# A gated attention and expert block: later groups measured before the token loop, the second norm scaled on ACT one step later

## The chip, the cores and the metric

The kernel runs on one core of a Trainium2 chip. The metric is the device time of one execution in microseconds, as the median of several runs. Engines are named as in the profile: PE multiplies matrices, DVE works on vectors, ACT applies functions, POOL (GpSimd) does small vector work and issues indirect transfers, and SP issues the plain ones.

## The reference, cut to what matters

Two residual blocks over 2048 tokens of width 256. The first is attention with 16 heads over a sliding window, whose keys and values come from a context; the second is a mixture of eight experts of which each token takes two. Each starts with a norm over the width, and each is gated by the tanh of one number:

```python
def _layernorm(x, axis=-1, eps=1e-05):
    m = jnp.mean(x, axis=axis, keepdims=True)
    v = jnp.var(x, axis=axis, keepdims=True)
    return (x - m) / jnp.sqrt(v + eps)

x = x + jnp.tanh(g_xattn[0]) * _L0_xattn_ref(_layernorm(x), ctx_1024, ctx_1024, wq, bq, wk, bk, wv, bv, wo, bo)
x = x + jnp.tanh(g_ffn[0]) * _L0_ffn_ref(_layernorm(x), ln_gamma, ln_beta, Wr, W12, W3)

# in _L0_ffn_ref, which norms its input once more:
xn = (xf - mu) / jnp.sqrt(var + 1e-05) * ln_gamma + ln_beta
logits = jnp.clip(xn @ Wr.T, -CLAMP, CLAMP)
probs = softmax(logits); top_p, top_i = jax.lax.top_k(probs, 2)
# each expert has a buffer of 640 slots; a token takes the next free one of each of its two experts
buf = jnp.zeros((E, cap, D)).at[e_s, pos].set(xn[t_s], mode='drop')
gu = einsum('ecd,efd->ecf', buf, W12); h = silu(gu[..., :D_FF]) * gu[..., D_FF:]
y = einsum('ecf,edf->ecd', h, W3)        # then weighted and added to the token's row
```

## The kernel before, in words

**Tiles and groups.** The tokens are cut into 16 tiles of 128 (`NB`), four tiles to a group (`NG` = 4 groups). One pass of the loop over `t` (L958) is called a step. It does the attention of tile t in three layers at once: it finishes tile t, whose scores were made one step earlier; it makes the scores of tile t + 1 and their exponents; and it takes tiles t - 1 and t - 2 through the output projection, the second norm and the router.

**A step, in the order written.** `summed(t, 1)` adds up the second half of the exponents (DVE, `sm`, L541). `divided(t - 1)` (L602 to L612) spreads the inverted sums over the heads on PE, copies them on ACT (`rb`) and multiplies on DVE (`oT`). `inverted(t)` (L543) takes the reciprocal on DVE (`rd`) and splits it on POOL into three parts of bf16 by four small operations (`rp`, L549 to L552). `scores(t + 1)` and `largest` follow (PE `ps`, DVE `mx`, L522), then `turned(t, 0)`: eight transposes on PE and two copies on ACT (`prT`, L563). Then, for t >= 2, `facing(t - 2)` transposes the normed tile (PE, `pxt`, L673) and `facing_read` copies it (ACT, `x2T`, L680). `attended(t - 1)` is the output projection (PE, L618). `attended_read(t - 1)` adds it to `x` on DVE (L631), takes mean and variance (L635, L637), and prepares the norm's factor: `ve` on DVE (L639), `rs`, its power of -1/2, on POOL (L643). After `turned(t, 1)` comes a unit of projection work for later tiles (`units(t)`, L730: keys, queries, values or turned rows, in one or two parts), the router's matmuls `routed(t - 2)` (L685) and `by_head(t)` (L575), which turns `rp` on PE; `by_head_read` copies it on DVE (`rdT`). `weighted(t)` (`po`, L591) is the product with the values.

**The second norm.** Near the end of step t, `scaled(t - 1)` subtracts the mean and multiplies by `rs` on DVE (`h2`, L650), then multiplies by gamma and adds beta on POOL (L659, L660). The last of these is returned as `normed`.

**The first norm of later groups.** Step t, for t = 1 to 8, measures one tile of group g + 2 (`measured`, L331: DVE bn_stats, bn_aggr, ve, and the power on POOL), and at its end scales it (`normed_x`, L345, `xn`) and adds the projection's bias to `x` (`biased`, L359, POOL).

**The router's sends.** When the slots of some tiles are known (`chosen`, `ranked`, `placed`, for tiles 0 to 2, 3 to 6, 7 to 10, 11 to 13 and 14, 15), each tile has two indirect transfers to make (`send`, L862, on POOL), 32 in all. `pace(normed, n)` (L949) issues up to n of them, queued behind `normed`. Three groups of tiles are sent within the loop; the rest follow it. The first expert's rows are fetched early by SP (L1027), after the sends that are out by step 12, and turned by the units `faced` (L700) in step 14.

**What sets the order.** The loop stands in `tc.manual_schedule(engines={PE, ACT, DVE})`: these three engines run their instructions as written. POOL and SP are ordered by a planner when the kernel is built; a send may not go ahead of its `normed`. PSUM banks for passing results come from one pool of three, taken in turn (`bank`, L90): a bank is reused as soon as the third one after it is asked for, and the taker waits until it was read.

**After the loop** (L1121 on), the last two tiles go through the same stations while PE starts on the first expert with the rows already fetched. The experts' part (from L1187) is not touched.

Of the kernel before, what the change touches and what calls it, by code (L numbers as in the profile page):

```python
# [20 lines left out]
P = 128  # L21
D = 256
DC = D // P
NB = 16
# [12 lines left out]
CAP = 640  # L37
# [18 lines left out]
def flamingo_block(  # L56
# [264 lines left out]
    with tc.tile_pool(name="grp", bufs=2) as grp, tc.tile_pool(  # L321
# [305 lines left out]
        def attended_read(t, pp):  # L627
            g, b = divmod(t, GB)
            x1 = xs[g][:, b, :]

            nc.vector.scalar_tensor_tensor(x1, pp, tgx[:, 0:1], x1, ALU.mult, ALU.add)  # L631


            st = small.tile([P, 6], F32, tag="st1", name=f"st1_{t}")
            nc.vector.bn_stats(st, x1)  # L635
            mv = small.tile([P, 2], F32, tag="mv1", name=f"mv1_{t}")
            nc.vector.bn_aggr(mv, st)  # L637
            ve = small.tile([P, 1], F32, tag="ve1", name=f"ve1_{t}")
            nc.vector.tensor_scalar(  # L639
                ve, mv[:, 1:2], 1.0 + LN_EPS, LN_EPS * LN_EPS, ALU.mult, ALU.add  # L640
            )
            rs = small.tile([P, 1], F32, tag="rs1", name=f"rs1_{t}")
            nc.gpsimd.tensor_tensor(rs, ve, minus_half[:, 0:1], ALU.pow)  # L643
            return mv, rs

        def scaled(t, mv, rs):
            g, b = divmod(t, GB)
            x1 = xs[g][:, b, :]
            h2 = wk.tile([P, D], F32, tag="h2", name=f"h2_{t}")
            nc.vector.tensor_scalar(  # L650
                h2, x1, mv[:, 0:1], rs[:, 0:1], ALU.subtract, ALU.mult
            )
            if b == 0:
                xn2s[g] = nrm.tile([P, GB, ROW], F32, tag="xn2", name=f"xn2_{g}")
                nc.gpsimd.tensor_copy(
                    xn2s[g][:, :, ROW - 1], tok_f[:, g * GB : (g + 1) * GB]
                )
            xn2 = xn2s[g]
            nc.gpsimd.tensor_tensor(h2, h2, ga_sb, ALU.mult)  # L659
            normed = nc.gpsimd.tensor_tensor(xn2[:, b, 0:D], h2, be_sb, ALU.add).ins  # L660
# [62 lines left out]
        def done(unit):  # L723
            parts, evict = unit
            for part in parts:
                part()
            return evict


        def units(t):  # L730
            g, b = divmod(t, GB)
            if t < GB:
                return [
                    lambda: unit_q(1, 0),
                    lambda: unit_q(1, 1),
                    lambda: unit_v(1, (0, 1)),
                    lambda: unit_k(2, 0),
                ][t : t + 1]
            if NB - 5 <= t < NB - 2:
                return [lambda: unit_v(g + (b + 1) // GB, ((t + 1) % GB,))]  # L740
            if t == NB - 2:
                return [lambda: faced((0, 1)), lambda: faced((2,))]
            if t == NB - 1:
                return [lambda: unit_v(g, (b,)), unit_none]
            return [
                [lambda: unit_k(g + 1, 1)],
                [lambda: unit_t(g + 1), lambda: unit_q(g + 1, 0)],
                [lambda: unit_v(g, (2, 3)), lambda: unit_q(g + 1, 1)],
                [lambda: unit_k(g + 2, 0), lambda: unit_v(g + 1, (0, 1))],
            ][b]  # L750
# [150 lines left out]
        with tc.manual_schedule(engines={PE, ACT, DVE}):  # L901
# [31 lines left out]
            nc.scalar.activation(tgx, gx_sb, AF.Tanh)  # L933
            for oc in range(DC):
                done(unit_q(0, oc))()
            sc = scores(0)
            for q in range(2):
                largest(0, q, sc)
# [19 lines left out]
            for t in range(NB):  # L958
# [4 lines left out]
                if t == 0:  # L963
                    prTs = turned(t, 0, sc)
                    parts, evict = unit_t(1)
                    parts[0]()
                    scn = scores(t + 1)
                    parts[1]()
                    evict()
                    summed(t, 1, sc)  # L970
                    rd = inverted(t, sc)
                    for q in range(2):
                        largest(t + 1, q, scn)
                else:
                    summed(t, 1, sc)
                    oT = divided(t - 1, *pend)
                    rd = inverted(t, sc)
                    if nxt:
                        scn = scores(t + 1)
                        for q in range(2):  # L980
                            largest(t + 1, q, scn)
                    prTs = turned(t, 0, sc)
                if t >= 1:
                    if t >= 2:
                        x2T = facing_read(t - 2, facing(t - 2))
                    norm = attended_read(t - 1, attended(t - 1, oT))
                if routing is not None:
                    place = placed(*ranked(*routing))
# [3 lines left out]
                ahead = t >= 1 and t - 1 < GB * (NG - 2)  # L992
                if ahead:
                    g, b = divmod(t - 1, GB)
                    mv_rs = measured(g + 2, [b])
                prTs += turned(t, 1, sc)
                parts, evict = work[0]()
                if len(work) > 1:
                    for part in parts:
# [8 lines left out]
                if t >= 2:  # L1008
                    routed_read(t - 2, pl)
                rdT = by_head_read(t, prd)  # L1010
                po = weighted(t, prTs, rdT)
                pend = po, rdT
                if t == 13:
                    next(choice)
                if routing is not None:
# [1 line left out]
                        pass  # L1017
                    waiting += of_tiles(*routing[0:2])
                    routing = None
                if t >= 1:  # L1020
                    normed = scaled(t - 1, *norm)

                    pace(normed, 3 if t < 11 else 4 if t < 13 else 2)
                if t == KNOWN:
                    assert not waiting
                    after_sent(
                        nc.sync.dma_start(  # L1027
                            rows_a,
                            slot_d[FIRST * CAP : FIRST * CAP + AS, :].rearrange(
                                "(s p) r -> p s r", p=P  # L1030
                            ),
                        ).ins
                    )
                if nxt:
                    exponents(t + 1, 0, H // 4 if t >= 1 else 0, H // 2, scn)
                    summed(t + 1, 0, scn)
                if ahead:
                    normed_x(g + 2, [b], *mv_rs)
                    biased(g + 2, [b])
                if t == KNOWN:  # L1040

# [615 lines left out]
```

## Time and profile before

| what | value |
|---|---|
| median of 3 runs | 509.55 us (509.44 to 509.55) |
| the profiled execution's own time | 510.99 us |
| its span, from first to last instruction | 509.3 us |
| busy PE / DVE / ACT / POOL | 479.6 / 300.3 / 226.4 / 173.0 us |
| the token loop, steps 1 to 15 | 33.1 to 182.4 us of the span |
| one step | 8.7 to 12.1 us |

Times in a profile are microseconds from the span's start. A line such as L643 is a line of the kernel's source. In a window's row, the first figure is its length; then come the busy time and number of instructions of PE, of PE's weight loads, of DVE, ACT and POOL, then the clock granted to PE (1.00 is full), the share of the DMA engines and their GB/s. In the timeline, brackets hold how long the engine had been idle and what released it.

### The profile page before, as it was taken

What the parts mean: (1) busy time and instruction counts of PE and PEld (TensorE: products, weight loads), DVE (VectorE), ACT (ScalarE), POOL (GpSimd) and SP (SyncE); (2) the same over time, 40 slices, a digit from 0 to 9 for tenths busy, and PEclk for the clock granted to TensorE, in tenths of its full rate; (3) what the DMA queues carried; (4) which work ended last, traced back from release to release, by engine and by line L of the source; (5) the groups of instructions that cost most, each with busy time, mean ns of one, the idle gap of its engine ahead of it and who ended that gap; (6) DMA issues with size and microseconds to landing.
All of it is one profiled execution on the core that took longest, in us unless ns stands there. A gap on an engine that the chain in (4) does not pass through costs nothing.

```text
span 509.3 us, 8874 instructions
## 1 busy us (share of the span) xinstructions
PE 479.6 (94%) x3095; PEld 364.9 (72%) x3095; DVE 300.3 (59%) x748; ACT 226.4 (44%) x650; POOL 173.0 (34%) x255
## 2 busy tenths in 40 slices
PE   9989999999988799999999999999999999999992
PEld 4556666667666566788887897987768776877682
DVE  6679997898779757125646373662663366235410
ACT  3689887688786633121221351422440344124300
POOL 6145434284265457302232322233110311034112
PEclk9999999999999999999999999999999999999998
DMA  8999610020022036401839472844700521024301
GB/s 254 328 278 390 235 43 1 2 82 27 1 86 77 18 102 229 160 2 25 308 64 305 116 232 37 267 91 82 266 10 5 130 51 12 4 35 108 132 14 41
DMA packets 38412, 59.21 MB, mean 116 GB/s; under 512 B 3616, under 2 KB 33824, under 8 KB 36192
## 3 DMA queue, kind: packets, MB, share of 16 engines
q1 hardware_dynamic: 30704, 47.71, 27.8%
q0 software_dynamic: 7056, 10.24, 10.6%
q8 instruction: 44, 0.72, 0.6%
q14 instruction: 64, 0.52, 0.4%
q10 hardware_dynamic: 544, 0.00, 0.1%
HBM read 39.40 MB, written 19.34 MB: 115 GB/s over the span
## 4 chain that ended last, share of the span: by engine, by line
PE 66%; DVE 12%; issue 7%; ACT 5%; DMA 5%; POOL 2%; SPq 0%; POOLq 0%; DVEq 0%; ACTq 0%
PE py L1399 16%; PE pg L1343 9%; PE pu L1343 7%; PE pu L1257 4%; PE pg L1257 4%; ACT pr L533 4%; DMA acc_d<-ysb,tok 4%; DVE sm L541 3%; PE pp L561 3%; DVE mx L522 3%; PE bank L1343 3%; PE pk L376 2%; PE pv L451 2%; PE ps L510 2%; PE pg L1090 2%
## 5 line engine op out<-in xcount | busy, mean ns | idle before, releaser
L1425 POOL DMA_INDIRECT acc_d<-ysb,tok x35 | 57.2, 1634 | 186.7 <-DMA acc_d<-ysb,tok 68.2
L1399 PE MATMUL py<-w,hT 128*128 128x256 f32 x432 | 97.1, 379 | 0.0
L1399 PEld LDWEIGHTS py<-w,hT 128*128 128x128 f32 x432 | 80.8, 190 | 11.3 <-DVE hT L1354 0.5
L533 ACT ACTIVATE pr<-ps,mx 128x128 f32<-128x128 f32 x256 | 69.9, 417 | 7.9 <-DVE mx L522 7.8
L1343 PE MATMUL pg<-bufT,w 128*128 128x320 f32 (+1 forms) x160 | 50.6, 398 | 0.2
L563 ACT COPY prT<-pp 128x512 f32<-128x512 f32 x64 | 35.0, 602 | 20.3 <-PE pp L561 20.1
L541 DVE TENSOR_REDUCE sm<-pr 128x8 f32<-128x1024 f32 x32 | 38.8, 1214 | 6.7 <-ACT pr L533 6.5
L1413 DVE TENSOR_SCALAR ysb<-py,rows 128x256 f32<-128x256 f32 x20 | 9.7, 484 | 55.0 <-PE py L1399 45.0
L1236 ACT COPY bufT<-bank 128x256 f32<-128x256 f32 (+1 forms) x42 | 11.4, 347 | 61.5 <-PE bank L1231 54.2
L522 DVE TENSOR_REDUCE mx<-ps 128x8 f32<-128x1024 f32 x32 | 36.7, 1188 | 3.4 <-PE ps L510 3.3
L561 PE MATMUL pp<-ident,pr 128*128 128x128 f32 x256 | 35.6, 282 | 0.3 <-DVE x_all L631 0.3
L1343 PEld LDWEIGHTS pg<-bufT,w 128*128 128x128 f32 x160 | 28.0, 189 | 10.7 <-ACT vp L1377 2.3
L561 PEld LDWEIGHTS pp<-ident,pr 128*128 128x128 f32 x256 | 29.5, 145 | 7.2 <-issue 4.8
L864 POOL DMA_INDIRECT slot_d<-xn,slot x32 | 31.7, 990 | 8.8 <-issue 7.0
L1374 ACT ACTIVATE vp<-pu 128x320 f32<-128x320 f32 (+1 forms) x40 | 15.8, 395 | 29.2 <-PE pu L1343 15.3
L1269 ACT ACTIVATE vp<-pg 128x256 f32<-128x256 f32 x24 | 9.2, 384 | 36.2 <-PE pg L1257 32.7
L1363 ACT COPY pg<-pg 128x320 f32<-128x320 f32 (+1 forms) x20 | 7.3, 367 | 33.6 <-PE pg L1343 29.0
L618 PE MATMUL pp<-wo_sb,oT 128*128 128x256 f32 x64 | 17.9, 403 | 4.3 <-DVE oT L612 2.9
L451 PE MATMUL pv<-wv_sb,ctx 128*128 128x256 f32 x64 | 17.8, 407 | 1.8 <-DVE x_all L631 1.4
L643 POOL TENSOR_TENSOR rs<-ve,minus_half 128x1 f32<-128x1 f32 x16 | 8.9, 558 | 27.9 <-DVE ve L639 26.3
L510 PE MATMUL ps<-keo,qT 32*128 32x256 f32 x256 | 18.4, 401 | 0.0
L591 PE MATMUL po<-prT,vp 128*32 128x128 f32 x512 | 17.4, 276 | 0.0
(227 smaller groups left out, 953.8 us busy)
## 6 DMA issues: line engine op xcount, KB each, us to landing
w<-in_w12T_dram SPq DMA_DIRECT2D x16, 1024.0 KB, 9.5
w<-in_w3T_dram SPq DMA_DIRECT2D x8, 1024.0 KB, 12.5
slot_d<-zrow SPq DMA_DIRECT2D x1, 5300.0 KB, 26.2
rows<-slot_d SPq DMA_DIRECT2D x7, 662.5 KB, 5.6
x_all<-in_x_dram SPq DMA_DIRECT2D x4, 512.0 KB, 6.5
acc_d<-x_all SPq DMA_DIRECT2D x4, 512.0 KB, 3.2
out_dram<-acc_d SPq DMA_DIRECT2D x4, 512.0 KB, 5.7
ctx<-in_ctxT_dram SPq DMA_DIRECT2D x3, 512.0 KB, 5.9
```

What stands on the lines that cost most here:

```text
L451: nc.tensor.matmul(pv[:, i, :], lhsT=cg[:, c, bs[i] * P : (bs[i] + 1) * P], rhs=wv_sb[:, c, :], start=(c == 0), stop=(c == DC - 1),)
L510: nc.tensor.matmul(pss[s // 2][:, s % 2, 2 * oc : 2 * oc + 2, :], lhsT=qT[rows, oc, b * P : (b + 1) * P], rhs=keo[rows, oc, b, :, :], star ...
L522: nc.vector.tensor_reduce(mx, sc[0][q], AX.X, ALU.max, negate=True)
L533: nc.scalar.activation(prs[q][:, i, j, :], pss[q][:, i, j, :], AF.Exp, bias=mxs[q][:, i, j : j + 1],)
L541: nc.vector.tensor_reduce(sc[3][:, q, :, :], sc[2][q], AX.X, ALU.add)
L561: nc.tensor.transpose(ppt[:, j, :], sc[2][q][:, i, j, :], ident)
L563: nc.scalar.copy(prT, ppt)
L864: d = nc.gpsimd.indirect_dma_start(out=slot_d, out_offset=bass.IndirectOffsetOnAxis(ap=slot[:, k, t : t + 1], axis=0), in_=xn2s[g][:, b, : ...
L1257: nc.tensor.matmul(ps, lhsT=w12[:, c, f0 : f0 + P], rhs=(buf[:, c, :, 0 : n // 2] if len(buf.shape) == 4 else buf[:, c, lo - off : hi - off]),
L1343: nc.tensor.matmul(to, lhsT=lhs[:, i * P : (i + 1) * P], rhs=rhs[:, 0:n], start=start, stop=True, skip_group_check=not start,)
L1399: mm = nc.tensor.matmul(py, lhsT=h, rhs=w3[:, f, :], start=(f == 0), stop=(f == FC - 1),)
L1425: nc.gpsimd.indirect_dma_start(out=acc_d, out_offset=bass.IndirectOffsetOnAxis(ap=tok[:, s : s + 1], axis=0), in_=ysb[:, s, :], in_offset= ...
```

## The change

The second norm's `ve` moves from DVE to POOL, which also computes a `shift` of minus mean times `rs`; `h2` becomes one activation on ACT with that shift and scale. `scaled` moves from the end of step t (for tile t - 1) to the beginning of step t + 1, with the sends that are queued behind it, and `facing` of that tile to a place behind the second `turned`. Groups 2 and 3 are measured whole, one ahead of the loop and one in step 0. Around these the number of sends per step, the fetch of the first expert's rows (from step 12 to step 13), the unit `faced((2,))` (from step 14 to step 15) and the order after the loop are fitted.

```diff
             ve = small.tile([P, 1], F32, tag="ve1", name=f"ve1_{t}")
-            nc.vector.tensor_scalar(
+            nc.gpsimd.tensor_scalar(
                 ve, mv[:, 1:2], 1.0 + LN_EPS, LN_EPS * LN_EPS, ALU.mult, ALU.add
             )
             rs = small.tile([P, 1], F32, tag="rs1", name=f"rs1_{t}")
             nc.gpsimd.tensor_tensor(rs, ve, minus_half[:, 0:1], ALU.pow)
-            return mv, rs
-
-        def scaled(t, mv, rs):
+            shift = small.tile([P, 1], F32, tag="shift", name=f"shift_{t}")
+            nc.gpsimd.tensor_scalar(shift, mv[:, 0:1], rs[:, 0:1], -1.0, ALU.mult, ALU.mult)
+            return shift, rs
+
+        def scaled(t, shift, rs):
...
-            nc.vector.tensor_scalar(
-                h2, x1, mv[:, 0:1], rs[:, 0:1], ALU.subtract, ALU.mult
-            )
+            nc.scalar.activation(h2, x1, AF.Identity, bias=shift[:, 0:1], scale=rs[:, 0:1])
...
             if t == NB - 2:
-                return [lambda: faced((0, 1)), lambda: faced((2,))]
+                return [lambda: faced((0, 1))]
             if t == NB - 1:
-                return [lambda: unit_v(g, (b,)), unit_none]
+                return [lambda: unit_v(g, (b,)), lambda: faced((2,))]
...
                 done(unit_q(0, oc))()
+            of_groups = {2: measured(2, every)}
             sc = scores(0)
...
                     summed(t, 1, sc)
                     oT = divided(t - 1, *pend)
+                    if t >= 2:
+                        normed = scaled(t - 2, *norm)
+
+                        pace(normed, 4 if KNOWN <= t < NB - 1 else 3)
+                    if t == KNOWN + 1:
+                        assert not waiting
+                        after_sent(
+                            nc.sync.dma_start(
+                                rows_a,
...
                     rd = inverted(t, sc)
...
                 if t >= 1:
-                    if t >= 2:
-                        x2T = facing_read(t - 2, facing(t - 2))
                     norm = attended_read(t - 1, attended(t - 1, oT))
...
-                    mv_rs = measured(g + 2, [b])
                 prTs += turned(t, 1, sc)
+                if t >= 2:
+                    x2T = facing_read(t - 2, facing(t - 2))
                 parts, evict = work[0]()
...
                 rdT = by_head_read(t, prd)
+                if t == 0:
+                    of_groups[3] = measured(3, every)
                 po = weighted(t, prTs, rdT)
...
-                if t >= 1:
-                    normed = scaled(t - 1, *norm)
-
-                    pace(normed, 3 if t < 11 else 4 if t < 13 else 2)
-                if t == KNOWN:
-                    assert not waiting
-                    after_sent(
...
                 if ahead:
-                    normed_x(g + 2, [b], *mv_rs)
+                    normed_x(g + 2, [b], *(m[:, b : b + 1] for m in of_groups[g + 2]))
                     biased(g + 2, [b])
...
             oT = divided(t, *pend)
-            x2T = facing_read(t - 1, facing(t - 1))
+            normed = scaled(t - 1, *norm)
+            pace(normed, 3)
             c = chosen(t - 4, 3)
             next(c)
             gate_or_up(0, 0)
             next(c)
             norm = attended_read(t, attended(t, oT))
+            x2T = facing_read(t - 1, facing(t - 1))
             silu(0)
```

More of the change, by code (lines that the diff above doesn't have):

```diff
@@ L976, in flamingo_block @@
                     oT = divided(t - 1, *pend)
+                    if t >= 2:
[6 more added lines that the diff above has]
+                                rows_a,
+                                slot_d[FIRST * CAP : FIRST * CAP + AS, :].rearrange(
+                                    "(s p) r -> p s r", p=P
+                                ),
+                            ).ins
+                        )
                     rd = inverted(t, sc)
@@ L1019, in flamingo_block @@
                     routing = None
-                if t >= 1:
-                    normed = scaled(t - 1, *norm)
-                    pace(normed, 3 if t < 11 else 4 if t < 13 else 2)
-                if t == KNOWN:
-                    assert not waiting
-                    after_sent(
[L1027 to L1033, printed above, removed]
                 if nxt:
```

## The prediction

> **What bounds the kernel now.** I read the page first (busy shares), then cut the token-tile loop into its sixteen steps and asked for the busy time of each, then followed the chain of waits through them, then read single steps in the timeline. A step t begins here where `divided(t - 1)` issues its matmuls (L602).
>
> ```profile
> PE 479.6 (94%) x3095; PEld 364.9 (72%) x3095; DVE 300.3 (59%) x748; ACT 226.4 (44%) x650; POOL 173.0 (34%) x255
> ```
>
> Over the whole span PE looks like the only bound, but the change touches only the first 190 us. There the steps differ. The windows below are steps 3, 6, 10, 12 and 15 (length, then busy time and instructions of PE, weight loads, DVE, ACT, POOL, then the granted clock):
>
> ```profile
> 51.05:59.70 8.65, 8.63 (x98) 5.82 (x98) 8.20 (x18) 7.28 (x25) 4.29 (x10) 1.00 0.95 339
> 79.31:90.84 11.53, 10.63 (x106) 7.31 (x106) 9.52 (x26) 8.12 (x27) 4.19 (x10) 1.00 0.01 2
> 122.44:133.16 10.72, 10.67 (x107) 7.32 (x106) 8.08 (x21) 8.04 (x27) 2.86 (x7) 1.00 0.00 0
> 142.48:152.60 10.12, 8.43 (x100) 6.07 (x99) 8.03 (x16) 7.88 (x27) 7.70 (x14) 1.00 0.32 108
> 172.79:182.44 9.65, 7.69 (x66) 6.31 (x66) 5.28 (x14) 5.34 (x17) 5.13 (x10) 0.82 0.08 28
> ```
>
> Steps 6 and 10 carry the same matmuls (their `units` are both V and Q). Step 10 is 10.72 us and all PE; step 6 is 11.53. The 0.8 us between them is DVE, as the chain in step 6 shows (start, time, what):
>
> ```profile
> 81.13 1.13 DVE sm L541
> 82.26 0.33 DVE oT L612
> 82.75 2.20 DVE mx L522 x2
> 84.95 0.40 DVE x_all L631
> 85.40 2.01 PE pv L451 x8
> ```
>
> So steps 1 to 3, 10 and the start of 11 are PE's; 4 to 8 and 13, 14 are lengthened by DVE. Step 12 is neither. In its timeline (start, duration, engine; in brackets the wait before) POOL issues four sends, and only then the casts of the inverted row sums (`rp`), though `rd` was there at 145.55; PE's turn of `rp` (L575) waits 1.33 us:
>
> ```profile
> 143.69 0.73 POOL L660 TENSOR_TENSOR xn<-h,be_sb 128x256 f32<-128x256 f32 x1
> 144.59 1.06 POOL L864 DMA_INDIRECT slot_d<-xn,slot  x1 [0.16 <-issue]
> 145.31 0.24 DVE L545 RECIPROCAL rd<-sm 128x16 f32<-128x16 f32 x1
> ...
> 148.49 0.96 POOL L864 DMA_INDIRECT slot_d<-xn,slot  x1 [0.30 <-issue]
> 149.45 0.21 POOL L549 CAST rp<-rd 128x16 bf16<-128x16 f32 x1
> 150.30 0.22 POOL L552 TENSOR_TENSOR rp<-rest,rp 128x16 bf16<-128x16 f32 x1
> 150.57 0.24 PE L575 MATMUL small<-ident_b,rp 128*48 128x128 bf16 x1 [1.33 <-POOL rp L552]
> ```
>
> **The change, part by part.**
>
> *Measuring groups 2 and 3 at once.* Removed from each of steps 1 to 8: on DVE bn_stats 0.41, bn_aggr 0.18, ve 0.15 (means of L337, L338, L340), 0.74 us; on POOL one pow of 0.56 to 0.73. Added twice: four pairs and one ve; for group 1 that took 12.83 to 15.25, 2.42 us, and its pow 1.01 on POOL. The first copy stands on DVE after group 1's scaling (ends 17.8) and before `mx` of tile 0, which starts at 21.07 after 3.30 us of idling: it ends at 20.2 if x's third load is there. That load is issued at 11.04 and these loads land 5.5 to 7.7 us later, so by 18.7; then 21.1 at worst: nothing. Without that idle time it would cost 2.4. The second copy stands behind tile 0's `rdT` (31.37), where DVE idles 1.06 and then 0.85 us: 2.42 - 1.91 = 0.5 us late for oT and mx of step 1, on the path: +0.5.
>
> *ve to POOL, shift added, h2 to ACT.* DVE loses 0.15 + 0.40 us a step, about 0.55. POOL gains two operations on 128x1; no such row exists. Between its 128x4 copy (0.19) and the 128x1 pow (0.56) I take 0.2 each, as the 128x16 casts cost. They are wanted only a step later: nothing on the path, up to 0.5 us a step more if POOL is full. h2 on ACT has no row either (a scale and a bias per partition from SBUF): the 128x256 copy L680 takes 0.40, the 512 wide one with bias L433 0.78; I take 0.40. It stands behind `rb`, where ACT then waits for PE's transposes anyway (L563 waits 20.1 us over 20 places; step 6: rb ends 80.56, the copy starts 81.91). Nothing; without that cover 14 x 0.4 = 5.6 us.
>
> *What DVE's relief is worth.* 1.3 us a step in 1 to 8, 0.55 later, but only until PE binds. By twins: step 4 to step 3, 0.3; step 6 to step 10, 0.8; step 5 to its twin step 9 (10.14), which itself still waits for DVE, 0.5 to 0.9, say 0.8; step 7 has no twin, 0.4; steps 11 and 14, 0.4 and 0.5. Sum -3.2. There is a rule to weigh: the Trainium skill (SBUF — State Buffer, "SBUF: two separate sides") says that DVE and GpSimd take a shared port pair exclusively for a whole instruction, where DVE runs a two-port mode or reads two SBUF operands. The row: `xn` L350 takes 0.40, but 0.71 while POOL adds beside it (59.40, 68.38). By the row each such meeting costs 0.3 us, and moving POOL's two 0.73 us operations from `xn`'s side to `sm` (1.20 to 1.22 in all 32) and PSUM reads spares perhaps 8 x 0.3 of DVE, 2.4 us; taken literally the lock could hold DVE for the whole 0.73. Neither changes my sum: steps 1 to 8 are then PE's.
>
> *The turn (facing) later in the step.* The same two transposes and one copy. attended comes 0.22 us sooner, facing now needs the bank that attended leaves (DVE's L631), as the unit did before. Where the unit is half a V (steps 11 to 13), its 0.4 us hardly cover x2T's copy: +0.3 us, hidden behind the next point. Zero to +1 in all; I take 0. `faced((2,))` goes from step 14 to 15, PE 0.44 us each way; the wait of 1.05 us for its bank (L673 for L711) may go: 0 to -1.
>
> *The sends move with h2.* Here I expect the loss. Sends are queued behind the norm's last add. Before, this add ran at the end of a step, so three sends were over soon in the next (step 8: 107.4, casts done 6.23 us into the step, PE's need at 7.17). PE, ACT and DVE keep their written order; POOL is ordered by a planner, but in every step of this trace where sends and casts meet, POOL kept the written order, and the new code writes scaled and sends ahead of `inverted`. From a step's beginning: rb ends at 1.2 to 2.5; h2 +0.4; the multiply +0.07; the add 0.81 later; from the add's start to the first cast 4.52 us with three sends (111.84 to 116.36), 5.76 with four (143.69 to 149.45); the casts 1.07. With the old rb ends (2.02, 2.19, 1.36, 1.95, 2.49) `rp` is ready at 8.9, 9.1 (steps 8, 9: three), 9.5, 10.1 (12, 13: four) and 9.4 (15: three), where L575 ran at 7.17, 7.04, 8.09, 7.34, 8.47. That is 1.7 + 2.0 + 1.4 + 2.7 + 0.9 = 8.7 us of PE waiting. ACT may run ahead during a wait, so rb could end at 1.2: then 5.9. I take 7. Behind L575 stand `po`, the unit's second half and the next step on PE, and on DVE `rdT` and all behind it: no cover. The SP load of rows_a goes behind step 13's sends; before it left at 160.19 and took 3.8, and `faced` reads it some 8 us into step 14: free.
>
> *After the loop.* h2, the two POOL operations and three sends stand before the last tile's ve; its turn, before at 191.77, comes some 0.7 us late; facing(14) gains about that in place of its 1.09 us wait. +0.3. The 14 last sends run unbroken from 190.72 to 208.2; 12 would run from about 9.8 us after step 15's end, done 25.0 after it (before 25.8): no new tail.
>
> *The clock.* The third kind of cost follows from the waits. Stretches of 3.41 us:
>
> ```profile
> 163.56:166.97 3.41, 2.08 (x27) 1.53 (x20) 3.20 (x11) 1.35 (x3) 0.29 (x1) 1.00 0.00 0
> 173.80:177.21 3.41, 1.45 (x9) 0.95 (x8) 2.41 (x4) 2.73 (x9) 2.86 (x4) 1.00 0.11 40
> 177.21:180.62 3.41, 3.41 (x14) 2.94 (x13) 1.25 (x4) 1.17 (x2) 1.70 (x6) 0.50 0.11 40
> ```
>
> A stretch with PE busy 2.08 us is followed by a full clock, one with 1.45 by half. The skill's TensorE: Matmul & The Clock Gate ("Why this matters for your kernels") allows gaps up to about 3 us: by it my waits cost no clock. By the row, whose longest single wait was 1.3 us, a wait of 1.7 to 2.7 can empty a stretch below 1.45; a halved one costs up to 1.7 us of PE. I go by the row: two or three such for the one there is, partly hidden in the next step's wait: +0.4 (0 to +4).
>
> **Sum** against the profiled run (510.99 us, span 509.3): +0.5 - 3.2 + 7 + 0.3 + 0.4 = +5.0, so 516.0; its median lies 1.44 below, so 514.5 for the median of 509.55.
>
> **Rivals.** (1) *Casts before sends*: the planner puts `rp` first because `rd` is ready within some tenths of h2. No wait arises, step 12 loses its own (10.12 to about 8.5), 8, 9, 13, 14 and 15 shorten by 0.4 to 1, the pxt wait and the halved stretch go: -3.2 - 1.3 - 3.5 + 0.8 + noise of the later turn 1.2 = -6: 503.5. It decides if the four casts issue before the first send. Against it: the order seen in steps 8, 9, 12, 13, 15. (2) *The wait swallowed*: order as forecast, but rb ends near 0.9 in every step and PE's need moves later; waits of 2.4 us and 0.8 for the beginning and the end against 3.2 gained: 509.5. (3) *ACT binds*: it is busy for up to 9.4 us of a step (step 9, of 10.1); if h2 finds no gap, 5.6 - 3.2: 512.
>
> **Numbers.** Forecast 0.70 (own range 511.5 to 518), rival 1 0.15, rival 2 0.10, rival 3 0.05. What a measurement tells from no change is 0.2%, 1.0 us. Rival 2 splits 0.04 faster, 0.03 same, 0.03 slower: faster 0.19, same 0.03, slower 0.78. Range 504 to 518: out are half of rival 1 and the forecast's upper tail.
>
> **What would show it.** Right: L575 waiting for L552 in steps 8, 9, 12, 13, some 7 us in all; sends before casts; DVE's sm, oT, mx gone from the chain in steps 4 to 7, step 6 near 10.7. Wrong: casts ahead of sends, or L563 and L618 late behind h2 on ACT.

## The result and the profile after

The changed kernel takes **523.41 us** (median of four runs, 522.22 to 523.95), the kernel before 509.55 (509.44 to 510.15): ratio **1.0276**, interval 1.0257 to 1.0296. It is slower by 13.9 us, where 5.0 were forecast; 523.4 lies outside the range of 504 to 518. Each time in this text is the median of a kernel's fast runs; the only slow run (530.94 us, of the kernel with h2 on ACT alone) is left out. The profiled execution of the changed kernel took 522.22 us, with a span of 520.5. It is the shortest of its four, and the profiled one of before (510.99) was longer than the others of before, so the two traces differ by only 11.2 us. That lies in the loop, which takes 11.4 us more: it starts at 33.16 (before: 33.11) and ends at 193.88 (before: 182.44). What follows it is 0.2 us shorter.

The page's busy shares of the changed kernel:

```profile
PE 484.5 (93%) x3095; PEld 367.1 (71%) x3095; DVE 291.7 (56%) x710; ACT 234.3 (45%) x666; POOL 176.3 (34%) x281
```

DVE lost 8.6 us of work and 38 instructions, ACT took 7.9, POOL 3.3. The work moved as intended, and the time still grew. Here are the same five steps as in the prediction (3, 6, 10, 12 and 15; windows of the changed kernel, with the same columns):

```profile
51.34:59.96 8.62, 8.45 (x98) 5.72 (x97) 6.66 (x12) 7.79 (x26) 3.96 (x11) 1.00 1.03 378
79.20:90.98 11.78, 10.59 (x107) 7.29 (x106) 8.40 (x21) 8.62 (x28) 4.09 (x11) 1.00 0.01 1
127.41:137.83 10.42, 10.25 (x106) 7.18 (x106) 6.93 (x14) 8.20 (x26) 3.23 (x9) 1.00 0.00 0
147.31:160.58 13.27, 10.00 (x100) 6.92 (x100) 8.17 (x19) 8.32 (x28) 7.48 (x14) 0.86 0.25 82
183.60:193.88 10.28, 6.56 (x68) 5.20 (x68) 4.39 (x11) 4.96 (x14) 6.32 (x12) 1.00 0.12 41
```

Step 6 has 1.1 us less of DVE's work (8.40 for 9.52) and is 0.24 us longer. Step 12 grew by 3.15 us. All fifteen steps, in us:

| steps | before | after | difference |
|---|---|---|---|
| 1 to 6 | 57.74 | 57.81 | +0.07 |
| 7 | 12.06 | 13.17 | +1.11 |
| 8, 9 | 19.55 | 23.27 | +3.72 |
| 10, 11, 14 | 31.07 | 30.84 | -0.23 |
| 12, 13 | 19.27 | 25.35 | +6.08 |
| 15 | 9.65 | 10.28 | +0.63 |

Steps 8, 9, 12, 13 and 15 are those with sends, and they hold 10.4 of the 11.4 us. Step 12 in the timeline of the changed kernel (start, duration, engine; in brackets the idle time before):

```profile
149.99 0.73 POOL L660 TENSOR_TENSOR xn<-h,be_sb 128x256 f32<-128x256 f32 x1
150.89 1.09 POOL L864 DMA_INDIRECT slot_d<-xn,slot  x1 [0.17 <-issue]
...
154.82 0.96 POOL L864 DMA_INDIRECT slot_d<-xn,slot  x1 [0.30 <-issue]
155.78 0.21 POOL L549 CAST rp<-rd 128x16 bf16<-128x16 f32 x1
...
156.63 0.22 POOL L552 TENSOR_TENSOR rp<-rest,rp 128x16 bf16<-128x16 f32 x1
156.90 0.30 PE L575 MATMUL small<-ident_b,rp 128*48 128x128 bf16 x1 [2.62 <-POOL rp L552]
157.24 0.17 DVE L695 TENSOR_SCALAR logits<-small 128x8 f32<-128x8 f32 x1 [3.84 <-PE small L575]
157.32 0.20 DVE L580 COPY rdT<-small 48x128 bf16<-48x128 bf16 x1
157.45 1.20 DVE L541 TENSOR_REDUCE sm<-pr 128x8 f32<-128x1024 f32 x1
```

The sends stand ahead of the casts, as forecast. `rp` is ready 9.54 us into the step (forecast 9.5), PE waits 2.62 us for it, and behind PE, DVE stands idle for 3.84 us. Waits of the loop, first before, then after (total us, number, longest):

```profile
DVE logits L695 <- PE small L575: 11.7, 11, 2.4
```

```profile
DVE logits L695 <- PE small L575: 32.6, 14, 3.8
PE small L575 <- POOL rp L552: 9.4, 5, 2.6
```

The wait at `logits` (L695) nearly tripled. It stands just behind the place where `measured` used to work, and it holds two things: PE's own waits for the casts, and DVE's relief, since DVE is done sooner and then waits for PE. The chain in step 6 of the changed kernel shows what it waits for:

```profile
82.65 2.20 DVE mx L522 x2
84.85 0.40 DVE x_all L631
85.26 0.14 issue
85.39 0.41 PE pxt L673 x2
85.80 1.74 PE pv L451 x8
```

The turn `pxt` now stands between `x_all` (L631) and the unit's matmuls, with 0.4 us on the chain, where it lay beside DVE's `mx` before. Last, the grid of 3.41 us around steps 12 and 13 (length, then busy time of PE, weight loads, DVE, ACT, POOL, then the granted clock):

```profile
153.33:156.74 3.41, 0.92 (x6) 0.52 (x4) 0.07 (x1) 3.39 (x13) 2.65 (x6) 1.00 0.81 266
156.74:160.15 3.41, 3.25 (x37) 2.43 (x37) 1.86 (x7) 0.00 (x0) 1.32 (x5) 0.50 0.03 12
160.15:163.56 3.41, 3.41 (x37) 1.55 (x35) 2.87 (x11) 1.32 (x5) 1.39 (x2) 0.50 0.00 0
166.97:170.38 3.41, 1.76 (x23) 1.20 (x27) 0.44 (x4) 3.41 (x14) 2.69 (x8) 1.00 0.29 97
170.38:173.79 3.41, 3.41 (x51) 1.74 (x44) 3.07 (x13) 1.31 (x6) 0.57 (x2) 0.50 0.46 117
```

The wait empties the stretch of 153.33 (PE busy 0.92 us), and the next two run at half clock; the wait of step 13 (stretch of 166.97, PE 1.76) does the same. Up to 200 us, five stretches are halved where one was; one of the five (from 194.27) lies behind the loop.

### The profile page after: what moved, and what is told of

Same layout as the page of the kernel before. It is cut to its first block, busy times and chain, and to the rows that moved or that the text cites. A ratio compares the mean times of both kernels' runs of the same rounds, so it can differ in the third digit from the quotient of the medians.

```text
span 520.5 us, 8910 instructions
## 1 busy us (share of the span) xinstructions
PE 484.5 (93%) x3095; PEld 367.1 (71%) x3095; DVE 291.7 (56%) x710; ACT 234.3 (45%) x666; POOL 176.3 (34%) x281
## 3 DMA queue, kind: packets, MB, share of 16 engines
q0 software_dynamic: 7056, 10.24, 10.5%
## 4 chain that ended last, share of the span: by engine, by line
PE 60%; DVE 14%; issue 8%; POOL 6%; ACT 5%; DMA 4%; SPq 0%; POOLq 0%; ACTq 0%; DVEq 0%
PE py L1403 17%; PE pg L1347 10%; PE pu L1347 7%; PE pu L1261 4%; PE pg L1261 4%; DVE mx L522 4%; DVE sm L541 3%; PE bank L1347 3%; POOL slot_d L864 3%; ACT pr L533 3%; PE pg L1092 2%; PE pu L1092 2%; PE bank L1235 2%; DMA bv_sb<-in_bv_dram 1%; DMA out_dram<-acc_d 1%
## 5 line engine op out<-in xcount | busy, mean ns | idle before, releaser
L1403 PEld LDWEIGHTS py<-w,hT 128*128 128x128 f32 x432 | 80.9, 190 | 11.2 <-DVE hT L1358 0.5
L1240 ACT COPY bufT<-bank 128x256 f32<-128x256 f32 (+1 forms) x42 | 11.4, 347 | 59.7 <-PE bank L1235 53.1
L1347 PEld LDWEIGHTS pg<-bufT,w 128*128 128x128 f32 x160 | 28.0, 190 | 10.7 <-ACT vp L1381 2.3
L659 POOL TENSOR_TENSOR h<-h,ga_sb 128x256 f32<-128x256 f32 x16 | 11.7, 731 | 36.6 <-ACT h L652 36.6
L695 DVE TENSOR_SCALAR logits<-small 128x8 f32<-128x8 f32 x14 | 2.3, 167 | 32.6 <-PE small L575 32.6
L510 PE MATMUL ps<-keo,qT 32*128 32x256 f32 x256 | 20.3, 435 | 0.0
L618 PE MATMUL pp<-wo_sb,oT 128*128 128x256 f32 x64 | 17.3, 394 | 3.2 <-DVE oT L612 3.0
L591 PE MATMUL po<-prT,vp 128*32 128x128 f32 x512 | 18.8, 290 | 0.0
```

What stands on the lines that cost most here:

```text
L510: nc.tensor.matmul(pss[s // 2][:, s % 2, 2 * oc : 2 * oc + 2, :], lhsT=qT[rows, oc, b * P : (b + 1) * P], rhs=keo[rows, oc, b, :, :], star ...
L1347: nc.tensor.matmul(to, lhsT=lhs[:, i * P : (i + 1) * P], rhs=rhs[:, 0:n], start=start, stop=True, skip_group_check=not start,)
L1403: mm = nc.tensor.matmul(py, lhsT=h, rhs=w3[:, f, :], start=(f == 0), stop=(f == FC - 1),)
```

## The experiments

The theory after the result: (a) the sends ahead of the casts cost what steps 8, 9, 12, 13 and 15 grew by, directly and through the clock; (b) the later turn lies on a ring from PE to DVE and back, and eats DVE's relief. The rival to (a): the waits are there, but slow clock is the larger cost. The rival to (b): measuring the groups ahead, or h2 on ACT, costs something itself. Each run is compared with the kernel before, run beside it on the same chip (the chips differ: there it took 515.92, 510.14 or 509.8 us). Steps are compared between traces; the trace of before is the one of the first section.

**The sends behind the casts.** Sends and the load of the first rows are queued behind the same step's `shift` instead of `normed`.

```diff
-                        pace(normed, 4 if KNOWN <= t < NB - 1 else 3)
...
                     norm = attended_read(t - 1, attended(t - 1, oT))
+                    if t >= 2:
+                        pace(shifted[-1], 4 if KNOWN <= t < NB - 1 else 3)
```

> The changed kernel with the sends of a step queued behind the norm's shift of the same step instead of behind its last add, so that the casts of rp and the ve, rs, shift stand ahead of them on POOL. Theory 1 (sends ahead of the casts hold PE at the turn of rp, and the holes halve the clock): the waits of L575 for L552, 9.8 us in six places, fall under 1 us, the five halved stretches of 3.41 us fall to one or two, and the time falls from 523.4 to 510 (508 to 513). Theory 2 (the later turn lengthens the ring DVE - PE - DVE of every step, and the sends only fill its holes): the time stays above 518.

Measured: 516.88 us beside 515.92, ratio 1.005 (1.0019 to 1.0081). PE's waits for the casts are gone but for one of 0.4 us; step 8 took 9.66 us, 9 10.24, 12 8.93 and 15 8.15. So this move alone takes back most of the loss (ratio 1.005 for 1.0276). It isn't clean, though: steps 10, 13 and 14 grew (11.71, 12.25 and 12.03 us), with waits that the trace ascribes to nothing in the core, in the window from 125 to 175 us:

```profile
ACT vp L466 <- remote: 5.2, 2, 3.4
```

What these are stays open; no other trace has them.

**PE kept busy during the waits.** Idle matmuls, whose output nobody reads, ahead of L575: 6, 6, 8, 8 and 4 in steps 8, 9, 12, 13 and 15.

```diff
+                for _ in range({8: 6, 9: 6, 12: 8, 13: 8, 15: 4}.get(t, 0)):
+                    nc.tensor.matmul(spare, lhsT=wo_sb[:, 0, 0:P], rhs=wo_sb[:, 1, :], start=True, stop=True)
                 by_head(t, rd, prd)
```

> The changed kernel with idle matmuls of 256 columns (six in steps 8 and 9, eight in 12 and 13, four in 15) put on PE ahead of the turn of rp, about 0.22 us each, so 1.3 to 1.8 us of work where PE waits 1.7 to 2.6 us; their output is not read. Theory 1: the waits' ends stay where they are, but the stretches are full, so the halved clock goes from five stretches to one or none and the time falls by 3 to 6 us, to 517.5 to 520.5. If the halved stretches lie in the shadow of the waits and cost nothing, or the holes are elsewhere: no change or up to 1 us slower.

Measured: 527.52 us beside 515.92, ratio 1.0247 (1.019 to 1.0305). A 32-bit matmul ran as two passes of 0.22 us, so the filling took up to 3.5 us and overran the wait: L575 moved from 9.2 to 10.1 in step 8, and steps 8 and 9 grew to 12.35 and 13.01 us. It decides nothing about the clock; the run with half of it, below, does.

**The groups measured whole, alone.** The kernel before with this part only.

```diff
+            of_groups = {2: measured(2, every)}
             sc = scores(0)
...
-                    mv_rs = measured(g + 2, [b])
...
+                if t == 0:
+                    of_groups[3] = measured(3, every)
...
-                    normed_x(g + 2, [b], *mv_rs)
+                    normed_x(g + 2, [b], *(m[:, b : b + 1] for m in of_groups[g + 2]))
```

> The kernel before with one part alone: groups 2 and 3 measured whole, one ahead of the loop, one in step 0; nothing else moves. The prediction's step (0.74 us of DVE a step off steps 1 to 8, worth some 2 us until PE binds): 507.5. Theory 1 as revised by the trace (DVE waits for PE at the logits, L695, right behind this work, so what is taken off before it only lengthens that wait): 509.0 to 510.0, with the wait of L695 for L575 grown by 3 to 6 us.

Measured: 515.65 us beside 515.92, ratio 0.9989 (0.9956 to 1.0022). The window from 33 to 100 us, before and with this part:

```profile
33.00:100.00 67.00, 63.04 (x674) 43.23 (x675) 59.38 (x136) 53.70 (x164) 27.60 (x60) 1.00 0.44 145
```

```profile
33.00:100.00 67.00, 62.93 (x685) 43.48 (x687) 56.10 (x120) 53.66 (x164) 23.76 (x54) 1.00 0.46 150
```

DVE does 3.3 us less in the same stretch, and PE no more: steps 4 to 7 are 8.96, 10.64, 11.53 and 12.06 us, to a hundredth those of before. (Step 1 grew by 0.23 us, for the second copy, and step 2 lost 0.26. In this one trace step 9 also grew by 1.74 us, with waits of ACT and DVE that it does not explain, and step 13 by 0.62; the median shows no such loss.) The relief ends as a wait at `logits`, whose total rose from 11.7 to 17.3 us. So in steps 4 to 7 more than half of the relief that the prediction counted, 0.74 of 1.3 us a step, was worth nothing.

**Two sends a step.** The changed kernel with two sends in steps 8, 9 and 10 instead of three in 8 and 9.

```diff
-                        pace(normed, 4 if KNOWN <= t < NB - 1 else 3)
+                        pace(normed, 4 if KNOWN <= t < NB - 1 else 2 if t < 11 else 3)
```

> The changed kernel with two sends instead of three in steps 8 and 9, and so two in step 10. A send takes 1.27 us of POOL. Theory 1: rp is ready 1.27 us sooner in steps 8 and 9 (at 7.9 and 7.4 us instead of 9.2 and 8.7), where PE wants it at about 7.2, and at about 7 in step 10, where PE wants it at 7.3: the time falls by 2.0 to 2.6 us, to 521. Theory 2: no change.

Measured: 522.6 us beside 515.92, ratio 1.0158 (1.0095 to 1.0221). Steps 8 and 9 fell by 1.26 and 1.27 us (10.19 and 10.55), step 10 grew by 0.30, in sum 2.2 us. A send's pitch on POOL is 1.26 to 1.27 us, so steps 8 and 9 move one for one with it: while PE waits for the casts, no cover lies over a send. (By the ratios this kernel gains more than 2.2 us, 5 to 6, but its interval is 3 us either way.)

**The changed kernel again**, unaltered, beside the next three.

> The changed kernel once more, unaltered, beside the next three on one chip. All theories: 2 to 3% slower than the kernel before, with waits of L575 for L552 of 9 to 10 us and four to six halved stretches of the clock.

Measured: 523.1 us beside 510.14, ratio 1.0254 (1.0203 to 1.0304). Every step but 13 and 14 was within 0.1 us of the first trace.

**Half the filling.** As above, with 3, 3, 4, 4 and 2 idle matmuls.

> The changed kernel with half as many idle matmuls as before (three in steps 8 and 9, four in 12 and 13, two in 15; each is two passes of 0.22 us, so 1.3, 1.7 and 0.9 us), which fit into the waits. Theory 1: the turn of rp stays at about 9.2, 8.7, 9.6, 9.2 us into steps 8, 9, 12, 13, the clock is full there, and what follows the turn in steps 12 and 13 takes 2.0 and 1.8 us again instead of 3.7 and 2.9: the time is 2 to 4 us under the changed kernel's. If the halved stretches cost nothing: the same as the changed kernel.

Measured: 525.88 us beside 510.14, ratio 1.0324 (1.0292 to 1.0355); its profiled execution took 522.32. The filling fits the waits this time: L575 stands at 9.22 us in step 8 and at 9.58 in step 12, as without it. Steps 12, 13 and 14, in the windows of this kernel and then of the changed one:

```profile
147.38:158.99 11.61, 10.19 (x108) 7.29 (x108) 7.66 (x15) 8.32 (x28) 7.47 (x14) 1.00 0.29 94
158.99:170.49 11.50, 9.85 (x107) 7.01 (x106) 7.49 (x24) 7.99 (x26) 7.29 (x13) 1.00 0.16 50
170.49:183.04 12.55, 10.05 (x109) 7.83 (x108) 9.67 (x28) 7.10 (x22) 3.34 (x9) 0.86 0.13 34
```

```profile
147.31:160.58 13.27, 10.00 (x100) 6.92 (x100) 8.17 (x19) 8.32 (x28) 7.48 (x14) 0.86 0.25 82
160.58:172.66 12.08, 10.27 (x99) 6.72 (x98) 8.24 (x24) 7.78 (x26) 7.29 (x13) 0.78 0.19 54
172.66:183.60 10.94, 10.31 (x108) 7.88 (x108) 8.13 (x26) 7.00 (x22) 3.28 (x9) 0.79 0.09 30
```

The clock is whole in steps 12 and 13, which are 1.66 and 0.58 us shorter, and what follows L575 in them takes 2.03 and 1.81 us, as in the kernel before (3.68 and 2.85 in the changed one). Step 14 is 1.61 us longer. DVE has 1.5 us more to do there (9.67 for 8.13). Some 1.1 us of it is work (`key` and most of a `sm`) that step 13 still held in the changed kernel; the rest is `mark` and `oh`, which now meet POOL's two operations of the second norm and take 0.70 and 0.39 us instead of 0.19 each. PE waits for DVE at the projection (L618, which is L621 here; over the whole trace the wait was 3.0 us in the changed kernel, the longest 1.6):

```profile
PE pp L621 <- DVE oT L615: 5.8, 5, 2.5
```

So the slow clock is real in steps 12 and 13, but DVE's work was waiting behind it. In this trace, taking the slow clock away gains 0.6 us over the three steps. The medians cannot test it: the other executions of this run took 525 to 528 us at a mean clock of .979 to .982 (the profiled one had .992), so the filling didn't always keep the clock up; why is open. The rival to (a) finds no support: the one execution with the whole clock gained next to nothing, while the runs that take the waits away gain most of the loss.

**The later turn, alone.** The kernel before with `facing` moved behind the second `turned`.

```diff
                 if t >= 1:
-                    if t >= 2:
-                        x2T = facing_read(t - 2, facing(t - 2))
                     norm = attended_read(t - 1, attended(t - 1, oT))
...
                 prTs += turned(t, 1, sc)
+                if t >= 2:
+                    x2T = facing_read(t - 2, facing(t - 2))
```

> The kernel before with one part alone: the turn of tile t - 2 (its two transposes and the copy) stands behind the second set of transposes instead of ahead of the projection; the norm, the sends and the groups stay. The prediction's step (same work, nothing to +1 us, taken as 0): 509.5 to 510.5, no step longer by more than 0.1 us. Theory 3 (in the steps that go round DVE - PE - DVE the turn now waits for x1 on DVE and then stands between it and the router's matmuls): steps 4 to 8 and 13, 14 grow by 0.2 to 0.5 us each and step 7 by more, the time by 1.5 to 3 us.

Measured: 513.75 us beside 510.14, ratio 1.0066 (1.0045 to 1.0088), so +3.4 us. Steps 2, 5, 6, 8, 9 and 10 each grew by 0.23 to 0.28 us, a little less than the 0.4 us that the two transposes take; steps 3 and 4 did not grow, and step 7 grew by 0.93. The wait that shows it, absent before:

```profile
PE pxt L673 <- DVE x_all L631: 5.9, 9, 0.8
```

The turn waits for the bank that `x_all` reads, and everything behind it on PE (unit, router, L575) comes later by the turn, DVE's `logits` and `rdT` too, and then the next step's `sm`. Step 12 also grew by 1.57 us, with a stretch at half clock in it (from 153.48); step 13 gave 0.49 back. So about 1 us of this cost comes with the slow clock of one step and not with the turn's own length.

**The casts first in the kernel before.** Sends queued behind the next step's casts, all else as before.

```diff
                     rd = inverted(t, sc)
+                    pace(parted[-1], 3 if t < 12 else 4 if t < 14 else 2)
...
-                    pace(normed, 3 if t < 11 else 4 if t < 13 else 2)
```

> The kernel before with its sends queued behind the last of the four casts of the next step, instead of behind the norm's last add; two stay at the end of step 15. Theory 1: step 12 loses its wait of 1.33 us for the casts (10.12 to 8.8), the other steps stay; 508 to 508.5, if the later sends do not hold back ve's power (rs) and with it h2 on DVE in steps 8, 9, 12 and 13. If they do, DVE stops there for h2 and these steps grow by 1 to 2 us each: 512 to 515.

Measured: 515.81 us beside 510.14, ratio 1.0107 (1.0077 to 1.0138). Step 12 lost its wait (8.72 for 10.12 us), as expected, but now the sends hold up `rs` and with it `h2`: step 9 took 11.77 us, 10 11.36 and 13 14.14. At both places tried on POOL, behind the norm's last add and behind the casts, the sends stand ahead of something that is needed soon.

**h2 on ACT, alone.** The kernel before with `ve` and `shift` on POOL and `h2` on ACT, at the old place.

```diff
-            nc.vector.tensor_scalar(
-                h2, x1, mv[:, 0:1], rs[:, 0:1], ALU.subtract, ALU.mult
-            )
+            nc.scalar.activation(h2, x1, AF.Identity, bias=shift[:, 0:1], scale=rs[:, 0:1])
```

> The kernel before with one part of the change: ve and shift on POOL, h2 on ACT, at its old place near the end of the step; turn, sends and measuring as before. Theory of the prediction (DVE's relief of 0.55 us a step counts wherever DVE lengthens the step): steps 5, 6, 7, 8, 9, 13, 14 shorten by 0.2 to 0.5 us each, about 2 us in all, ratio 0.996. Rival (ACT's h2 at the end of a step stands ahead of the exponents of the next half tile and delays sm, or DVE waits elsewhere): no step shorter by more than 0.2 us, ratio 1.000 to 1.005.

Measured: **524.0 us** beside 509.8, ratio 1.0265 (1.0237 to 1.0293). Neither theory expected this; by the ratio it is 13.5 us. Steps 2, 3 and 4 grew by 1.5 to 1.7 us each (10.56, 10.15 and 10.46). The end of step 2 in its timeline:

```profile
50.48 0.27 POOL L645 TENSOR_SCALAR shift<-mv,rs 128x1 f32<-128x1 f32 x1
50.78 0.60 ACT L652 ACTIVATE h<-x_all,shift,rs 128x256 f32<-128x256 f32 x1 [0.91 <-POOL shift L645]
51.29 3.18 ACT L533 ACTIVATE pr<-ps,mx 128x128 f32<-128x128 f32 x12
52.44 1.22 DVE L541 TENSOR_REDUCE sm<-pr 128x8 f32<-128x1024 f32 x1 [1.60 <-ACT pr L533]
54.52 0.43 PE L497 MATMUL ps<-band,ident_b 32*32 32x512 bf16 x14 [1.40 <-ACT pr L533]
```

At the end of a step h2 stands ahead of the exponents in ACT's order. It waits 0.91 us for the shift and takes 0.60; that makes the exponents 1.5 us late, then `sm`, and then PE's next scores, which need the bank the exponents read. PE's wait there, in the loop of before and of this kernel:

```profile
PE ps L497 <- ACT pr L533: 2.1, 4, 0.8
```

```profile
PE ps L497 <- ACT pr L533: 16.0, 16, 1.7
```

The loop of this trace is 17.4 us longer, and this wait grew by 13.9. The rest, half clock in steps 9 and 12 to 15 among it, was not taken apart. So moving h2 to the next step's beginning is what makes it free on ACT. The changed kernel needs that move, and the sends, queued behind the norm, went with it to a place ahead of the casts.

**Both reliefs at their old places.** The run above plus the groups measured whole.

> The run above and groups 2 and 3 measured whole as well; turn and sends at their old places. These two parts are the whole relief of DVE. Theory of the prediction: 3.2 us less than before and 0.5 for the copy in step 1, ratio 0.995; step 6 near 10.7 us. Rival (PE's turn of the inverted sums and the matmuls before it hold DVE's logits, so relief ends as a wait there): ratio 0.998 to 1.003, steps 5 to 7 within 0.4 us of before.

Measured: 526.91 us beside 509.8, ratio 1.0348 (1.0322 to 1.0373). The measuring repairs nothing: steps 2 to 4 are 10.61, 10.23 and 10.50 us.

**The sends at their old place, all else changed.** The changed kernel with sends and load written at the end of the step again.

```diff
-                        pace(normed, 4 if KNOWN <= t < NB - 1 else 3)
...
                     routing = None
+                if t >= 2:
+                    pace(shifted[-1], 3 if t < 11 else 4 if t < 13 else 2)
+                if t == KNOWN:
+                    assert not waiting
+                    after_sent(
```

> The changed kernel with the sends and the load of the first rows written where they were before (end of the step, same numbers of sends), queued behind the shift; h2 on ACT at the step's beginning, the later turn and the measuring stay. If the sends ahead of the casts cost 7.4 us and the later turn 3.4: no L575 wait on POOL's casts over 1.4 us, steps 8, 9, 12 and 15 near 9.7, 10.4, 10.1 and 9.8, total 3 to 4 us above before, ratio 1.006 to 1.009. If the late placement of h2 has a cost of its own besides sends and turn: above 1.010.

Measured: 512.91 us beside 509.8, ratio 1.0051 (1.0032 to 1.007). The longest waits of its loop hold those at `logits` and of the turn (the lines are numbered six higher in this kernel), but the one at L575 for the casts is gone:

```profile
DVE logits L701 <- PE small L575: 23.8, 14, 2.6
...
PE pxt L679 <- DVE x_all L631: 5.1, 9, 0.8
```

Steps 8, 9, 12 and 13 are 9.68, 9.94, 10.17 and 9.13 us, within 0.3 of before. Step 14 is not: it took 13.59 us (before 11.04) at a mean clock of 0.77, and step 15 8.11 (9.65); this trace is of one of the longer executions. The kernel differs from the changed one in the sends alone, that is their place, their number per step and the load behind them: 1.0254 or 1.0276 against 1.0051 is **10.3 to 11.5 us for the sends**. The 2.6 us that remain are the other parts together, and the turn alone had cost 3.4. So DVE's whole relief comes out at some 0.8 us. Each of the two figures is uncertain by about 1 us, so this is not told from nothing; 2.7 us, as forecast with the copy's cost, it is not. The trace shows a part of it in step 5: 10.92 us with the turn alone, 10.29 here and in the changed kernel.

**Three and five sends.** The kernel before, with one send of step 12 put into step 13.

```diff
-                    pace(normed, 3 if t < 11 else 4 if t < 13 else 2)
+                    pace(normed, 3 if t < 12 else 5 if t < 13 else 2)
```

> The kernel before with three sends queued at the end of step 11 and five at the end of step 12 in place of four and four. Step 12 has one send less ahead of its casts (1.27 us earlier, its wait of 1.33 us at L575 gone), step 13 one more (casts end 8.1 us into the step in place of 6.83, PE wants them at 7.34, so a new wait of 0.7 us). Expected: step 12 8.9 us (from 10.12), step 13 9.9 (from 9.15), total 0.5 us less, ratio 0.999. If a wait of PE for the casts costs nothing because DVE binds: both steps unchanged.

Measured: 509.5 us beside 509.8, ratio 0.9999 (0.9982 to 1.0016). Step 12 took 8.86 us, as expected; step 13 took 11.98 in place of 9.9, and step 14 9.65 in place of 11.04. The grid around step 13's wait:

```profile
156.74:160.15 3.41, 2.01 (x16) 1.63 (x14) 2.36 (x6) 3.24 (x12) 2.81 (x7) 1.00 0.34 122
160.15:163.56 3.41, 3.41 (x37) 2.10 (x37) 2.94 (x12) 2.10 (x9) 1.44 (x3) 0.53 0.45 106
```

The new wait is followed by a slow stretch, which the expectation left out, and DVE does part of step 14's work meanwhile. The sum of steps 12 to 14 is 30.49 us, before 30.31. None of these versions beats the kernel before.

## Why the prediction was right or wrong

**The sends (+7): right in place and mechanism, and in size for the wait itself.** The prediction gave, step by step, when `rp` would be ready. It came as follows:

| step | forecast | measured | L575 before | later by |
|---|---|---|---|---|
| 8 | 8.9 | 9.16 | 7.17 | 2.04 |
| 9 | 9.1 | 8.67 | 7.04 | 1.68 |
| 12 | 9.5 | 9.54 | 8.09 | 1.50 |
| 13 | 10.1 | 9.17 | 7.34 | 1.89 |
| 15 | 9.4 | 8.68 | 8.47 | 0.26 |

L575 issues 0.05 to 0.06 us after `rp`; "later by" is its own delay. The sum is 7.37 us. Rivals 1 and 2 fall with it, since the last casts came behind the sends in all five steps (in step 9 the first of the four went ahead, which gained nothing) and the waits are of the full size. Rival 3 falls as well: with the sends out of the way, all the other parts cost 2.6 us, less than the turn alone, so h2's work on ACT costs nothing visible. With what came behind the waits (3.1 us, below) the sends make 10.5 us of the trace, which agrees with the 10.3 to 11.5 of the runs.

**What DVE's relief is worth (-3.2): this step failed.** By the step's twins the prediction took the difference of two steps as DVE's and so as what relief would return. The run with the groups alone gives 0.0 in steps 4 to 7, and all the relief with the sends out of the way comes out at some 0.8 us, not told from nothing. The prediction's own sign did not come: step 6 took 11.77 us instead of 10.7, with `mx` still on its chain. The error was in where the removed work stood. `measured` filled time in which DVE was about to wait for PE's L575 anyway, while what makes the steps long, `sm`, `oT`, `mx` and the choice's operations, stands on the other side of that wait. The wait at `logits` was in the trace of before, with 11 places and 11.7 us; the prediction didn't read it.

**The turn later in the step (0, from 0 to +1): this step failed too.** Alone it costs 3.4 us. The prediction counted the same instructions and one bank wait and called them hidden. But PE's part from `x_all` to L575 lies in series between DVE's `x1` and DVE's `logits`, and a turn put into it lengthened six steps by 0.23 to 0.28 us each, step 7 by 0.93, and step 12, with half clock, by 1.57.

Together these two make +0.95 us in the trace outside the steps with sends (step 7 alone +1.1), where the prediction had -3.2 + 0.5 = -2.7, all of it in these steps. Only step 5 became clearly shorter, by 0.35 us of the 0.8 forecast. In step 7 there is also a collision that the prediction named with the wrong sign: POOL's h2 operations left `xn` and met `upto`. Step 7 of the changed kernel:

```profile
92.73 0.73 POOL L659 TENSOR_TENSOR h<-h,ga_sb 128x256 f32<-128x256 f32 x1 [1.09 <-ACT h L652]
92.79 0.69 DVE L799 TENSOR_TENSOR upto<-sofar,sums 128x8 f32<-128x8 f32 x1
```

`upto` takes 0.17 us in the trace of before, without POOL beside it, and 0.69 here. It ends as POOL's operation does, so the 128x8 row is held for nearly all of it. Step 7 ended only 0.2 us later than with the turn alone, though (12.99 us there, 13.17 here). Such a row stood in the trace of before:

```profile
90.78 0.72 POOL L361 TENSOR_TENSOR x_all<-x_all,bog 128x256 f32<-128x256 f32 x1 [0.60 <-DVE xn L350]
90.82 0.72 DVE L789 TENSOR_TENSOR mark<-key,top 128x24 f32<-128x24 f32 x1
```

The next operations of this size took 0.18 us there. Both rows are what the Trainium skill's SBUF — State Buffer ("SBUF: two separate sides") says taken literally, which the prediction weighed and set aside for the milder row of `xn` (0.40 to 0.71).

**The clock (+0.4, 0 to +4): mis-sized as taken, within its bounds.** From L575 to the step's end, step 12 took 3.68 us (before 2.03), step 13 2.85 (1.81) and step 15 1.55 (1.18), which is 3.1 us. The 2.7 of steps 12 and 13 are the halved stretches, since with the clock whole these parts took 2.03 and 1.81 us again. The choice to go by the row and not by the Trainium skill's TensorE: Matmul & The Clock Gate ("Why this matters for your kernels") was right: a stretch with a longest wait of 2.62 us was followed by half clock. But the prediction expected the next wait to hide most of it; here the slow stretch falls into the time after the wait. And the filled run showed the reverse side: with the clock whole, most of this time was lost to DVE in step 14.

**h2 on ACT (0): right at the new place, for a reason that was half seen.** It takes 0.60 to 0.76 us, not 0.40, and still hides behind the wait for the transposes. The prediction's price without cover, 5.6 us, counted h2's own time alone. At the old place it is 13.5 us by the ratio, because ACT keeps its written order and the next exponents then wait for POOL's shift too; the prediction did not ask what stands behind h2.

**The rest.** The second copy of the measuring cost 0.23 us in step 1 (0.5 forecast), and the time after the loop fell by 0.2 (+0.3 forecast). So the forecast +5.0 became +11.2 in the traces: 7.4 for the waits, 3.1 behind them, 0.95 in all other steps, and -0.2 after the loop. The medians differ by 2.7 us more, which no trace shows.

## What to carry to other kernels

Before counting a relieved engine as gain, find where in its order the removed work stood, and look for the wait just behind it: here relief ahead of a wait for another engine came back as a longer wait, and that wait could be read in the trace of before. Treat an in-order engine as a list of who stands behind whom: moving an operation moves all that is queued behind it, and here one small move of the norm carried three or four sends of 1.27 us each in front of four casts of 0.2 us that the whole next step needed. A slow clock behind a wait isn't a cost of its own until a run has shown that filling the wait shortens the total.

## What was not expected of the hardware

- An activation on ACT from SBUF with a scale and a bias per partition took 0.60 us, up to 0.76, for 128x256, where the copy of the same size from PSUM (L680) takes 0.37 to 0.40.
- The half clock came after stretches of 3.41 us with PE busy 0.92, 1.45, 1.76 and (as 0.53) 2.01 us. It did not come after one with 2.08 in the kernel before, nor in the changed one after the first and the third of these rows (each has its follower below it), so the busy time of such a stretch does not decide it:

```profile
122.60:126.01 3.41, 1.99 (x37) 1.41 (x37) 1.42 (x4) 3.41 (x14) 2.52 (x7) 1.00 0.22 80
126.01:129.42 3.41, 3.41 (x41) 1.71 (x40) 3.12 (x11) 1.75 (x5) 0.38 (x1) 1.00 0.02 5
184.04:187.45 3.41, 1.82 (x12) 1.46 (x11) 2.57 (x4) 2.73 (x8) 1.45 (x2) 1.00 0.00 0
187.45:190.86 3.41, 2.75 (x19) 2.29 (x17) 1.09 (x3) 1.78 (x5) 2.66 (x3) 1.00 0.21 78
```

- A DVE operation on 128x8 took 0.69 us instead of 0.17 while POOL multiplied beside it, and one on 128x24 took 0.72 beside POOL's add.
- POOL's operations on 128x1 took 0.19 (`ve`) and 0.26 to 0.27 us (`shift`).
